# Two graph-attention and mixture-of-experts layers: rows scattered into expert regions while they are routed, engines in written order

## The chip, the cores and the metric

The kernel runs on one core of a Trainium2 chip. The metric is the device time of one execution in microseconds. The core has TensorE (PE, its weight loads shown apart as PEld), VectorE (DVE), ScalarE (ACT), GpSimd (POOL) and SyncE (SP); SP and POOL issue the transfers, which 16 DMA engines carry out.

## The reference, cut to what matters

There are 2708 rows of 256 features and a 2708 x 2708 adjacency. Every layer is an attention over the graph followed by a mixture of experts, each added to its input:

```python
# layer 0
x = x + gat(layernorm(x), adj)       # softmax over neighbours of leaky_relu(s_i + s_j), times h
x = x + moe(layernorm(x))            # 8 experts, 256 -> 1024 -> 256, gelu
# layer 1
x = x + hyperbolic_gat(layernorm(x), adj)   # W_gcn, W_att, per-row arccosh/sinh scalars, elu, sigmoid
y = n + moe(n), n = layernorm(x)     # 16 experts, 256 -> 512 -> 256, relu
x = x + layernorm(y) * gamma + beta
```

```python
def moe(x):                          # top-2 of E experts
    top_w, top_i = top_k(x @ Wg + bg, 2); top_w = softmax(top_w)
    return sum over k of top_w[k] * (act(x @ W1[top_i[k]] + b1) @ W2[top_i[k]] + b2[top_i[k]])
```

## The kernel before, in words

The rows are 22 tiles of 128 (the last has 20), used as 11 pairs. `x_all` holds them on the chip all the time.

Attention 0 (loop at L772 to L808). For each row tile, `mask_row` (DVE, L700) turns a row of the adjacency, loaded two tiles ahead, into a bf16 mask; `mask_turn` transposes it on PE (L709) and casts it on ACT (L712) into `mask_t`. For each pair and each source tile, `weigh` makes the weights (`zr` on ACT L722, `z` on DVE L725) and `gather` multiplies them on PE (L735). `close0` divides and adds; `turn0` applies the second layer norm, writes the row tile to DRAM (`rows_d`, SP, L357), transposes it, and `gate` gives the logits (L364).

The mixture of experts (`experts`, from L426). When all logits are there, a plan is computed at once for all rows: the two best experts by compares and reduces (L429 to L441), the rank of each row within its expert by products with a triangle matrix and with ones (L451, L455) and a scan (L461), the place of each row in blocks of 128 rows of one expert (L492 to L518), and the inversion, which gives for each place the row that goes there: 44 compares `in_block` (L523), each with a PE product (L525) with `which`. From it come `comes` and `goes`, the rows to read and the slots to write (L533 to L539). Biases are turned (L555), and `b2`, weighted by the gates, is added to every tile by a transpose (`wt_ps`, L567), a copy (L569), a product (`b_ps`, L571) and an add on DVE (L572). Then one loop over blocks (50 in layer 0, 58 in layer 1): `load` fetches the expert's weights on SP and the 128 rows by an indirect DMA on POOL (L589, three buffers); `hidden` transposes the rows, multiplies (L601) and applies the activation on ACT (L603); `outputs` multiplies (L611), copies on DVE (L614) and scatters to `outs_d` on POOL (L615). Lastly the combine loop fetches both results of each row as `two` (L640) and adds them, weighted (L645), to the accumulator.

Between the layers. `ready1` loads `w_gcn`, `W_att` and `a1_j` once the experts of layer 0 are done, and multiplies them into `w1x` (L846, L852). `project1` (L858) then takes each combined group through the layer norm, a transpose and a product with `w1x`. Per-row scalars follow for all tiles at once (L226 to L248), then attention 1 (L936 to L987): `widen` casts half a mask row on ACT (L938), `sum_up` multiplies (L946), `finish1` applies the elu. The sigmoid stage follows (L995, L998, L1004), the layer norm and routing rows of layer 1 (L1014 to L1021), the second mixture, and `finish` (L1023 to L1047), which normalizes each combined group of four tiles and writes it out.

What sets the order: a scheduler arranges the instructions of every engine by its own estimates of when their inputs are ready, within the order that the data allow. Groups of four tiles serve for the layer norms of L1014 and of the finish.

Of the kernel before, what the change touches and what calls it, by code (L numbers as in the profile page):

```python
# [32 lines left out]
def kernel(  # L33
# [25 lines left out]
    nc = tc.nc  # L59
    N, D = x.shape  # L60
# [6 lines left out]
    groups = [tiles[g:g + 4] for g in range(0, T, 4)]  # L67
# [62 lines left out]
    l0_scope = ExitStack()  # L130
    l0_pool = l0_scope.enter_context(tc.tile_pool(name="l0", bufs=1))
# [24 lines left out]
    nc.gpsimd.memset(minus_one, -1.0)  # L156
    nc.gpsimd.memset(mask_t[:, TF, :], 1.0)
# [13 lines left out]
    def score_weights():  # L171
        for c in range(DC):
            for k, (av, coef) in enumerate(((a0[1], 0.2), (a0[1], 0.8), (a0[0], 0.8))):
                junk = row_tile("junk", 2)
                nc.vector.scalar_tensor_tensor(
                    junk, w0_t[:, c, :D], coef, av, op0=OP.mult, op1=OP.mult,
                    accum_out=w0_t[:, c, D + k:D + k + 1])
# [6 lines left out]
    b2_0 = l0_pool.tile([E0, D], F32, name="b2_0")  # L184
    nc.gpsimd.dma_start(b2_0, L0_ffn_b2)
    b2_1 = const.tile([E1, D], F32, name="b2_1")
    nc.gpsimd.dma_start(b2_1, L1_ffn_b2)
    gamma = broadcast_rows("gamma", L1_ffn_gamma, 0, D)
    beta = broadcast_rows("beta", L1_ffn_beta, 0, D)
    b1_0 = l0_pool.tile([E0, L0_ffn_b1.shape[1]], F32, name="b1_0")  # L190
    nc.gpsimd.dma_start(b1_0, L0_ffn_b1)
# [115 lines left out]
    def ln_stats(ln, src, group):  # L307
# [7 lines left out]
        v, s, q = (stat()[:, :n] for _ in range(3))  # L315
        nc.vector.tensor_scalar(v, mv[:, lo:lo + n, 1], LN_EPS, None, op0=OP.add)
        nc.scalar.activation(s, v, AF.Sqrt)
        nc.vector.reciprocal(q, s)
        nc.vector.tensor_tensor(q, q, v, OP.mult)
        nc.vector.tensor_tensor(q, q, s, OP.add)  # L320
        nc.vector.tensor_scalar(q, q, 0.5, None, op0=OP.mult)
        nc.vector.reciprocal(rstd[:, lo:lo + n], q)
# [9 lines left out]
    def transpose_rows(dst, src, r):  # L332
# [4 lines left out]
        nc.scalar.copy(dst, ps[:, :DC, :r])  # L337
# [8 lines left out]
    class Router:  # L346


        def __init__(self, layer, E, w_gate, b_gate):
# [11 lines left out]
        def gate(self, t, r):  # L361
            ps = ps_wide("gate_ps")
            project(ps[:r, :self.E], self.xt.pop(t), self.w_gate, r)
            nc.vector.tensor_tensor(self.logits[:r, t, :], ps[:r, :self.E], self.b_gate[:r],  # L364
                                    OP.add)

# [710 lines left out]
```

## Time and profile before

| | us |
|---|---|
| median of three runs | 1458.45 (1456.02 to 1458.71) |
| profiled execution | 1459.07, its span 1457.3 |
| attention 0, PE without a gap | 30.5 to 332.7 |
| plan of layer 0 | 332.7 to 400.5 |
| expert blocks of layer 0 (50) | 400.5 to 765.4 |
| weights of layer 1, first `two` | 765.4 to 785.5 |
| combine, projection | 785.5 to 847 |
| scalars, mean | 847 to 885.5 |
| attention 1 | 885.5 to 1009.5 |
| sigmoid, scalars | 1009.5 to 1064 |
| rows, plan of layer 1 | 1064 to 1167.5 |
| expert blocks of layer 1 (58) | 1167.5 to 1389.8 |
| combine, finish | 1389.8 to 1457.3 |

PE is busy 81% of the span, DVE 40%, ACT 47%, POOL 16%; 248.46 MB are moved by DMA. Stages were read off the trace by the first and last instruction of each loop. The lines "busy tenths in 40 slices" cut the span into slices of 36.4 us, a digit of 9 is 90% or more; PEclk is the TensorE clock that was granted, in tenths. A line of windows gives, for one stretch, the busy time of each engine with the number of its instructions, the clock, the share of DMA and its rate.

### The profile page before, as it was taken

Reading aid. Unit: us, or ns where it says so; the run is one execution under the profiler, and the core shown is the slowest. Engines: PE = TensorE matmul, PEld = TensorE weight load, DVE = VectorE, ACT = ScalarE, POOL = GpSimd, SP = SyncE. Lnnn points to the kernel's source line nnn. Section 1 sums busy time; section 2 is a strip of 40 time slices with the busy share of each in tenths; the row PEclk is TensorE's granted clock in tenths of the full one; section 3 lists DMA queues with packets and bytes.
Section 4 is the critical chain, followed back from the end, with each engine's and each line's share of the span. In section 5 each row is a group of like instructions: output and inputs, shape, how many; then the busy total and the mean of one; then the engine's idle time right before and its main releaser. Section 6 shows DMA issues by size and latency. Waiting matters only on the chain. (4 is left out here: it accounts for less than half of the span.)

```text
span 1457.3 us, 21300 instructions
## 1 busy us (share of the span) xinstructions
PE 1184.7 (81%) x7294; PEld 1002.1 (69%) x7294; DVE 589.2 (40%) x1905; ACT 681.4 (47%) x1632; POOL 236.4 (16%) x297
## 2 busy tenths in 40 slices
PE   3999999993899999999992929997052999999910
PEld 2778888852599999999991408996051599999810
DVE  4756566637300000000004765566468501111179
ACT  3877777741144444444431546664611144444400
POOL 4000000000022222222211100000000045555400
PEclk9999999996599999999996969998555599999965
DMA  7313333000299999999963200000010199999943
GB/s 263 144 46 129 122 130 122 21 8 5 76 344 323 328 327 326 327 327 327 327 216 109 65 0 1 1 1 1 0 58 19 37 319 354 353 352 342 327 143 98
DMA packets 145181, 248.46 MB, mean 170 GB/s; under 512 B 9351, under 2 KB 102302, under 8 KB 142366
## 3 DMA queue, kind: packets, MB, share of 16 engines
q1 hardware_dynamic: 134354, 218.39, 43.3%
q0 software_dynamic: 10720, 28.72, 6.3%
q8 instruction: 58, 0.95, 0.3%
q14 instruction: 49, 0.40, 0.1%
HBM read 224.60 MB, written 22.47 MB: 170 GB/s over the span
## 5 line engine op out<-in xcount | busy, mean ns | idle before, releaser
L601 PEld LDWEIGHTS hid_ps<-xg_t,w_b 128*128 128x128 f32 x2528 | 301.3, 194 | 10.9 <-ACT xg_t L337 4.7
L611 PE MATMUL out_ps<-w_b,ht 128*128 128x256 f32 x1264 | 308.1, 380 | 0.0
L601 PE MATMUL hid_ps<-xg_t,w_b 128*128 128x128 f32 x2528 | 304.2, 277 | 1.8 <-ACT xg_t L337 1.0
L603 ACT ACTIVATE ht<-hid_ps,bias 128x128 f32<-128x128 f32 x632 | 232.2, 368 | 149.6 <-PE hid_ps L601 114.9
L614 DVE COPY yo<-out_ps 128x256 f32<-128x256 f32 x108 | 45.9, 425 | 548.2 <-PE out_ps L611 548.2
L735 PE MATMUL att_ps<-g_all,z 128*128 128x257 f32 x968 | 245.8, 391 | 0.6 <-DVE z L725 0.6
L611 PEld LDWEIGHTS out_ps<-w_b,ht 128*128 128x128 f32 x1264 | 224.3, 191 | 22.0 <-issue 0.2
L735 PEld LDWEIGHTS att_ps<-g_all,z 128*128 128x128 f32 x968 | 165.2, 185 | 42.6 <-issue 13.5
L589 POOL DMA_INDIRECT xg<-rows_d,comes x108 | 104.5, 967 | 477.8 <-PE tr_ps L336 314.6
L722 ACT ACTIVATE zr<-e_bc,minus_one,g_all 128x256 f32<-128x256 f32 (+1 forms) x242 | 139.9, 590 | 53.8 <-DVE z L725 52.0
L725 DVE SCALAR_TENSOR_TENSOR z<-zr,mask_t 128x256 f32<-128x256 f32 (+1 forms) x242 | 99.2, 410 | 92.5 <-PE att_ps L735 79.2
L946 PE MATMUL att_ps<-half,wide_mask 128*128 128x258 f32 x968 | 124.2, 287 | 0.0
L946 PEld LDWEIGHTS att_ps<-half,wide_mask 128*128 128x128 f32 x968 | 118.3, 188 | 6.2 <-issue 0.4
L615 POOL DMA_INDIRECT outs_d<-yo,goes x108 | 106.7, 988 | 71.4 <-issue 36.9
L337 ACT COPY xg_t<-tr_ps 128x256 f32<-128x256 f32 x108 | 40.2, 372 | 166.4 <-PE tr_ps L336 166.3
L468 POOL MEMSET edge<- 128x9 f32 (+1 forms) x2 | 0.2, 111 | 530.5 <-PE att_ps L735 314.0
L938 ACT CAST wide_mask<-mask_t 128x1408 fp32r<-128x1408 fp8e4 x44 | 59.9, 1368 | 45.2 <-PE att_ps L946 45.2
L712 ACT CAST mask_t<-mt_ps 128x1024 fp8e4<-128x1024 bf16 (+2 forms) x66 | 57.1, 871 | 24.4 <-PE mt_ps L709 24.2
L336 PE MATMUL tr_ps<-ident,y_all 128*128 128x128 f32 (+1 forms) x44 | 13.2, 426 | 62.9 <-DVE y_all L326 62.8
L709 PE MATMUL mt_ps<-ident_bf,mb 128*128 128x128 bf16 (+1 forms) x484 | 42.2, 226 | 17.8 <-DVE mb L700 16.8
L709 PEld LDWEIGHTS <-mb 128*128 128x128 bf16 (+1 forms) x484 | 34.3, 102 | 29.8 <-DVE mb L700 17.7
L336 PEld LDWEIGHTS tr_ps<-ident,y_all 128*128 128x128 f32 (+1 forms) x44 | 8.9, 251 | 63.8 <-DVE y_all L326 58.0
(288 smaller groups left out, 1179.3 us busy)
## 6 DMA issues: line engine op xcount, KB each, us to landing
w_b<-in_L_ffn_W_dram SPq DMA_DIRECT2D x100, 1024.0 KB, 9.3
w_b<-in_L_ffn_w_dram SPq DMA_DIRECT2D x116, 512.0 KB, 6.3
ad<-in_adj_dram SPq DMA_DIRECT2D x21, 1354.0 KB, 5.8
two<-outs_d SPq DMA_DIRECT2D x42, 256.0 KB, 2.9
rows_d<-xn SPq DMA_DIRECT2D x21, 128.0 KB, 1.7
rows_d<-y_all SPq DMA_DIRECT2D x21, 128.0 KB, 1.7
out_dram<-xn SPq DMA_DIRECT2D x21, 128.0 KB, 1.7
xg<-rows_d,comes POOLq DMA_INDIRECT x108, 6.1
```

Source lines behind the costliest of these rows:

```text
L589: nc.gpsimd.indirect_dma_start(out=xg, out_offset=None, in_=rows_d[:, :], in_offset=bass.IndirectOffsetOnAxis(ap=comes[:, b:b + 1], axis=0))
L601: nc.tensor.matmul(ps[:, :P], w1_b[:, c, f * P:(f + 1) * P], xt[:, c, :], start=(c == 0), stop=(c == DC - 1))
L603: nc.scalar.activation(ht[:, f, :], ps[:, :P], func, bias=bias[:, f, b:b + 1])
L611: nc.tensor.matmul(ps[:, :D], ht[:, f, :], w2_b[:, f, :], start=(f == 0), stop=(f == FC - 1))
L615: ins = nc.gpsimd.indirect_dma_start(out=outs_d[:, :], in_=yo, in_offset=None, out_offset=bass.IndirectOffsetOnAxis(ap=goes[:, b:b + 1], a ...
L709: nc.tensor.transpose(ps[:w, k, :r], mbs[i][:r, c * P:c * P + w], ident_bf[:r, :r])
L712: nc.scalar.copy(mask_t[:, lo:lo + full, i * P:i * P + r], ps[:, :full, :r], saturate=False)
L722: nc.scalar.activation(zr[:k, :n], e_bc[:k, lo:lo + n], AF.Relu, bias=minus_one[:k], scale=g_all[:k, j, D + 1:D + 2])
L725: nc.vector.scalar_tensor_tensor(z[:k, :n], zr[:k, :n], 1.0, mask_t[:k, j, lo:lo + n], op0=OP.add, op1=OP.mult)
L735: nc.tensor.matmul(accs[i][:r, :D + 1], z[:k, q * P:q * P + r], g_all[:k, j, :D + 1], start=(j == 0), stop=(j == TF))
L938: nc.scalar.copy(m, mask_t[:, part * HALF:(part + 1) * HALF, i * P:(i + 1) * P])
L946: nc.tensor.matmul(accs[i][:, :D + 2], wide_masks[i, j // HALF][:k, j % HALF, :], half[:k, j, :], start=(j == 0 and half is halves[0]), st ...
```

## The change

The order of PE, ACT, DVE and SP is now the order in which the program is written (`manual_schedule`); POOL's is still arranged. The program is rewritten to suit: `pipeline` runs the steps of successive pairs staggered, and attention 0 has an agenda that says after which of its steps each piece of other work is issued.

Routing is done pair by pair. In layer 0 the routing of a pair runs within the attention of the next one; in layer 1 it is a pipeline of six steps after the sigmoid stage. `pick` finds the two best experts, `rank` counts by three small products, `number` adds a running count per expert, and four indirect DMAs on POOL scatter the rows of the pair, each with its row and pair number in two extra columns (258 columns), into a region of 2816 rows per expert in DRAM. As the regions are only partly written, they are first filled with zeros by `clear` on SP: 22 fills of 9 x 128 rows of 1032 bytes (1.189 MB each) in layer 0, two behind each of the first eleven loads of the adjacency, and 22 of 17 x 128 rows (2.246 MB each) in layer 1, issued before attention 1.

The plan that remains computes for each block its expert and its first row in that expert's region; `comes` is a run of rows with a bound, so nothing is inverted. The slots to write are read from the extra columns of the gathered rows, two small DVE operations per block. The transposes and products of `b2` move into the first 22 blocks of the expert loop. The first two blocks are loaded ahead of the loop, `xg` has four buffers, and the weights of layer 1 are loaded and multiplied before the expert blocks of layer 0. Combine, projection and finish go by pairs, with `two` fetched two pairs ahead. The layer norm takes the square root with its epsilon on ACT and a correction step on DVE, per pair. In attention 1 the next mask is widened after the products of the present one. Attention 0 starts its first pair after 8 of the 22 front steps and has six buffers of z with a lag of four.

```diff
+    ctx.enter_context(tc.manual_schedule(engines={ET.PE, ET.Activation, ET.DVE, ET.SP}))
...
+    def pipeline(items, *steps):
+        for n in range(len(items) + len(steps) - 1):
+            for k in reversed(range(len(steps))):
+                if 0 <= n - k < len(items):
+                    steps[k](items[n - k])
...
-    def ln_stats(ln, src, group):
...
+    def ln_head(ln, src, group):
...
+        nc.scalar.activation(rstd[:, lo:lo + n], mv[:, lo:lo + n, 1], AF.Sqrt, bias=eps)
...
+        nc.vector.reciprocal(q, rstd[:, lo:lo + n])
+        nc.vector.tensor_tensor(w, q, q, OP.mult)
+        nc.vector.scalar_tensor_tensor(w, mv[:, lo:lo + n, 1], LN_EPS, w,
+                                       op0=OP.add, op1=OP.mult)
+        nc.vector.tensor_scalar(w, w, -0.5, 1.5, op0=OP.mult, op1=OP.add)
+        nc.vector.tensor_tensor(rstd[:, lo:lo + n], q, w, OP.mult)
...
-            self.rows_d = dram.tile([N, D], F32, name=f"rows_d{layer}")
...
-            nc.sync.dma_start(self.rows_d[t * P:t * P + r, :], xn)
...
+            self.rows_d = dram.tile([(E + 1) * LIMIT, RW], F32, name=f"rows_d{layer}")
...
+        def clear(self, k):
+            view = self.rows_d.rearrange("(e t p) d -> t p e d", e=self.E + 1, p=P)
+            for t in range(2 * k, 2 * k + 2):
+                ins = nc.sync.dma_start(
+                    view[t], nobody.unsqueeze(1).to_broadcast([P, self.E + 1, RW]))
+                for other in self.moves:
+                    tc.declare_no_dep(ins.ins, other, reason="a pair's tokens do not come that far")
+                self.fills.append(ins.ins)
...
+        def pick(self, pair):
+            E, lo, n = self.E, pair[0][0], len(pair)
+            hi = lo + n
+            order = rank[E].unsqueeze(1).to_broadcast([P, n, E])
+            seen = self.logits[:, lo:hi]
+            for k in range(2):
+                m = self.top[k]
+                nc.vector.tensor_reduce(m[:, lo:hi], seen, AX.X, OP.max)
...
+            both = row.tile([P, n, E], BF16, name="both", tag=f"both{E}", bufs=2)
+            nc.gpsimd.tensor_tensor(both, self.hot[:, lo:hi, 0], self.hot[:, lo:hi, 1], OP.add)
+            self.both = both
+            for t, r in pair:
+                nc.gpsimd.tensor_copy(self.rows[t][:r, D:D + 2], self.first[:r, t])
+        def rank(self, pair):
+            E, lo, n = self.E, pair[0][0], len(pair)
+            hi = lo + n
+            bank = ps_wide("rank_ps")
+            ps = bank[:, :2 * n * E].rearrange("p (t k e) -> p t k e", k=2, e=E)
+            sums = bank[:, 256:256 + n * E].rearrange("p (t e) -> p t e", e=E)
+            nc.tensor.matmul(ps, tri, self.hot[:, lo:hi], start=True, stop=False)
+            nc.tensor.matmul(ps[:, :, 1], ones_bf, self.hot[:, lo:hi, 0], start=False, stop=True)
+            nc.tensor.matmul(sums, ones_bf, self.both, start=True, stop=True)
+            self.ps[lo] = ps, sums
+        def number(self, pair):
+            E, lo, n = self.E, pair[0][0], len(pair)
+            hi = lo + n
+            ps, sums = self.ps.pop(lo)
+            at = row.tile([P, n, 2, E], F32, name="before", tag=f"before{E}", bufs=2)
+            for q in range(n):
+                nc.vector.tensor_tensor(at[:, q], ps[:, q],
+                                        self.count.unsqueeze(1).to_broadcast([P, 2, E]), OP.add)
+                nc.vector.tensor_tensor(self.count, self.count, sums[:, q], OP.add)
+            nc.vector.tensor_tensor(at, at, self.hot[:, lo:hi], OP.mult)
+            with nc.allow_low_precision(reason="whole numbers below 2 ** 24"):
+                nc.vector.tensor_reduce(self.place[:, lo:hi], at, AX.X, OP.add)
+            for t, r in pair:
+                for k in range(2):
+                    ins = nc.gpsimd.indirect_dma_start(
+                        out=self.rows_d[:, :], in_=self.rows[t][:r], in_offset=None,
+                        out_offset=bass.IndirectOffsetOnAxis(ap=self.place[:r, t, k:k + 1],
+                                                             axis=0))
+                    for other in self.moves:
+                        tc.declare_no_dep(ins.ins, other, reason="rows of different pairs")
+                    self.moves.append(ins.ins)
+                del self.rows[t]
...
-        in_block = gates.tile([P, G, P], BF16, name=f"in_block{layer}")
-        which = gates.tile([P, G, 2, NB], BF16, name=f"which{layer}")
-        nc.vector.tensor_tensor(which[:, :, 1, :], iota_b.unsqueeze(1).to_broadcast([P, G, NB]),
-                                place[:, 0].unsqueeze(2).to_broadcast([P, G, NB]), OP.is_equal)
-        nc.vector.tensor_tensor(which[:, :, 0, :], which[:, :, 1, :],
-                                tile_of.unsqueeze(2).to_broadcast([P, G, NB]), OP.mult)
-        for k in range(2):
-            nc.vector.tensor_scalar(which[:, k * T:(k + 1) * T, 1, :],
-                                    which[:, k * T:(k + 1) * T, 1, :],
-                                    pair_no[:, k:k + 1], None, op0=OP.mult)
-        ps = ps_wide("pair_ps")
-        for g in range(G):
-            nc.vector.tensor_scalar(in_block[:, g, :], iota_p, place[:, 1, g:g + 1], None,
-                                    op0=OP.is_equal)
-            nc.tensor.matmul(ps[:, :2 * NB], in_block[:, g, :],
-                             which[:, g].rearrange("p c b -> p (c b)"),
-                             start=(g == 0), stop=(g == G - 1))
...
-            ps = ps_wide("wt_ps")
-            nc.tensor.transpose(ps[:E, :r], wts[:r, t, :], ident[:r, :r])
-            wt = row.tile([E, P], F32, name=f"wt{layer}")
-            nc.scalar.copy(wt[:, :r], ps[:E, :r])
...
+        nc.vector.tensor_scalar(jump, need, -float(P), float(LIMIT), op0=OP.mult, op1=OP.add)
+        nc.gpsimd.memset(step_e, 2.0 ** 22)
+        nc.gpsimd.tensor_tensor(step_e[:, :E - 1], router.count[:, 1:], router.count[:, :E - 1],
+                                OP.subtract)
+        nc.gpsimd.tensor_scalar(end, router.count[:, 0:1], -1.0, None, op0=OP.add)
+        passed(row_f, jump)
+        passed(bound, step_e)
+        nc.vector.tensor_tensor(row_f, row_f, slots[:, :NB], OP.add)
+        nc.vector.scalar_tensor_tensor(comes, bound, end, row_f, op0=OP.add, op1=OP.min)
+        nc.vector.scalar_tensor_tensor(inside, bound, end, row_f, op0=OP.add, op1=OP.is_ge)
...
+            xg = pool.tile([P, RW], F32, name="xg", bufs=4)
+            ins = nc.gpsimd.indirect_dma_start(
+                out=xg, out_offset=None, in_=rows_d[:, :],
+                in_offset=bass.IndirectOffsetOnAxis(ap=comes[:, b:b + 1], axis=0))
+            for other in router.moves + router.fills:
+                tc.add_manual_dep(ins.ins, other.name, LANDED, reason="any pair's row")
+            return w1_b, w2_b, xg
...
+        held = [load(b) for b in range(2)]
...
+            goal = pool.tile([P, 1], I32, name="goal", bufs=3)
+            nc.vector.scalar_tensor_tensor(goal, xg[:, D + 1:D + 2], mine[:, b:b + 1],
+                                           xg[:, D:D + 1], op0=OP.not_equal, op1=OP.add)
+            nc.vector.copy_predicated(goes[:, b:b + 1], full[:, b:b + 1], goal)
...
+        aside()
+        xts, late = {0: turn(held[0][2])}, None
         for b in range(NB):
-            w1_b, w2_b, xg = load(b)
-            ht = hidden(b, w1_b, xg)
+            if b + 2 < NB:
+                held.append(load(b + 2))
+            w1_b, w2_b, xg = held.pop(0)
+            ht = hidden(b, w1_b, xts.pop(b))
+            if b + 1 < NB:
+                xts[b + 1] = turn(held[0][2])
             if late is not None:
                 outputs(*late)
-            late = (b, w2_b, ht)
+            late = (b, w2_b, xg, ht)
+            if 1 <= b <= T:
+                b2_add(*tiles[b - 1])
+            if b < T:
+                b2_turn(*tiles[b])
+                b2_evict(*tiles[b])
...
+        pipeline(pairs, fetch, lambda pair: None, combine, *after)
...
+        if i < len(pairs):
+            router0.clear(i)
...
+        steps = [(0, close0, pair), (2, lambda p: ln_tail(ln_f0, p), pair)]
+        for q, tl in enumerate(pair):
+            steps += [(3 + q, lambda p: turn0(*p), tl),
+                      (4 + q + LAG, lambda p: router0.evict(*p), tl)]
+        steps += [(7 + LAG, router0.gate, pair), (8 + 2 * LAG, router0.take, pair),
+                  (8 + 2 * LAG, router0.pick, pair), (12 + 2 * LAG, router0.rank, pair),
+                  (12 + 3 * LAG, router0.number, pair)]
...
+    LAG, FRONT = 4, 8
...
+    def load_weights(pool):
+        room = pool.tile([P, DC, 1024], F32, name="w1_b").rearrange("p c f -> p (c f)")
+        parts = {}
+        for name, lo, n in (("w_gcn", 0, D), ("w_gcn_t", 512, D), ("att_x", 1024, D + 1)):
+            parts[name] = room[:, lo:lo + DC * n].rearrange("p (c f) -> p c f", f=n)
+        parts["a1_j"] = room[:, 1600:1600 + D]
...
+        router1.clear(k)
...
+    widen(FIRST, 0)
+    widen(FIRST, 1)
     for i in range(FIRST, T):
-        for part in range(2):
-            widen(i, part)
-        finish1(*tiles[i - FIRST])
         for j in range(T):
             sum_up(i, j)
-    for i in range(T - FIRST, T):
-        finish1(*tiles[i])
+        if i + 1 < T:
+            widen(i + 1, 0)
+            widen(i + 1, 1)
+        if i == FIRST:
+            for old in range(FIRST - 1):
+                finish1(*tiles[old])
+        finish1(*tiles[i - 1])
+    finish1(*tiles[T - 1])
...
+    pipeline(pairs, lambda p: ln_head(ln_f1, x_tile, p), rows2, gate2, pick2, router1.rank,
+             router1.number)
...
+    def finish(pair):
+        ln_tail(ln_y, pair)
+        for t, r in pair:
+            o = row_tile("xn", 4)
+            ln_apply(o[:r], y_all[:r, t, :], ln_y, t, r)
             nc.vector.tensor_tensor(o[:r], o[:r], gamma[:r], OP.mult)
             nc.vector.tensor_tensor(o[:r], o[:r], beta[:r], OP.add)
             nc.vector.tensor_tensor(o[:r], o[:r], x_all[:r, t, :], OP.add)
             nc.sync.dma_start(out[t * P:t * P + r, :], o[:r])
```

## The prediction

> **What bounds the kernel now.** I read the page's slices first, to find the stages, then the windows cut along them, then the chain of waits for the two planning stages. From the page, busy tenths in 40 slices of 36.4 us, and the share of DMA:
>
> ```profile
> PE   3999999993899999999992929997052999999910
> DVE  4756566637300000000004765566468501111179
> PEclk9999999996599999999996969998555599999965
> DMA  7313333000299999999963200000010199999943
> ```
>
> PE is full in slices 1 to 8 (attention 0), 11 to 20 (FFN 0), 24 to 27 (attention 1) and 32 to 37 (FFN 1). Between them the granted clock falls to 0.5 and nothing is full: these are the stages that the change rewrites. The windows; columns are stretch, length, busy time of PE, PEld, DVE, ACT and POOL, clock, DMA share, GB/s:
>
> ```profile
> 0.00:39.00 39.00, 15.18 (x94) 11.60 (x94) 18.61 (x69) 14.64 (x26) 15.83 (x47) 1.00 0.77 273
> 115.00:165.00 50.00, 50.00 (x304) 41.91 (x303) 32.16 (x91) 37.81 (x69) 0.00 (x0) 1.00 0.37 135
> 333.00:399.30 66.30, 39.44 (x143) 23.84 (x142) 40.75 (x146) 9.90 (x37) 3.19 (x5) 0.52 0.11 36
> 540.00:610.00 70.00, 70.00 (x481) 65.34 (x480) 4.25 (x10) 31.60 (x86) 18.07 (x19) 1.00 0.93 330
> 765.00:785.00 20.00, 4.85 (x12) 3.23 (x12) 0.94 (x5) 2.68 (x5) 3.22 (x7) 0.66 0.19 56
> 785.00:847.00 62.00, 46.07 (x132) 21.38 (x132) 48.97 (x187) 26.51 (x119) 6.50 (x23) 0.89 0.29 85
> 1102.00:1167.00 65.00, 36.16 (x127) 20.98 (x124) 45.03 (x131) 8.65 (x30) 2.92 (x3) 0.50 0.08 27
> 1240.00:1310.00 70.00, 70.00 (x491) 65.18 (x490) 7.64 (x18) 34.64 (x94) 36.70 (x38) 1.00 1.03 354
> 1390.00:1457.30 67.30, 0.00 (x0) 0.00 (x0) 59.27 (x212) 1.23 (x6) 0.85 (x2) 0.53 0.41 126
> ```
>
> Both planning stages (333 to 399, 1102 to 1167) are serial work on DVE and PE with the DMAs idle. FFN 0 is PE's (70 of 70). FFN 1 is PE's and the DMAs' together (70 of 70, 354 GB/s). The last stage is DVE's (59 of 67). The chain of waits names what each planning stage ends with, and what follows FFN 0:
>
> ```profile
> 768.93 8.15 DMA w_gcn<-in_L_gnn_W_gcn_dram
> 1148.60 5.41 PE b_ps L571 x12
> 1155.18 4.56 PE b_ps L571 x10
> 1161.48 4.71 DMA xg<-rows_d,comes
> ```
>
> So the b2 products and then the first gather (4.71 us) end the plan, and a weight load of 8.15 us stands behind FFN 0. The sum below is against the profiled execution: 1459.07 us, span 1457.3, 1.8 around it; the median of the runs is 0.6 less.
>
> **Plan 0 (332.7 to 400.5, 67.8 us): -36.** Removed from this path: 44 in_block compares with their matmuls, the two which products, the scan, b2. What stays after the last attention matmul, in order: the rank and number of pair 9, which written order puts ahead of the last close, delay it by 2.1; close, LN, transposes, gate and logits 6.7 (10 or so dependent steps of 0.2 to 0.5 with one table load of 1.28); pick 2.4 (12 small DVE steps at 0.2); rank 1.0; number 1.2 (6 steps); four scatters on POOL at 0.97 and about 2.2 to land (5 us in all for one at 1389.8: issue 0.97, the fetch behind it starts 2.6 after), 6.1; gather 1.0 + 4.7; transpose and copy 1.2. That is 26.4. The bias transposes (5.3 in before) and the w_gcn products (1.08 + 3.77 in before) are written ahead of the first block on PE; about half falls beside the scatters and gather: 5 to 6. So 32 in place of 67.8. Bounds: 26 if all of it hides, 42 if none does and the weights for block 0 (9.3 from issue to landing, after the plan) come last. On SP the loads of b2, b1, w_gcn, W_att and a1_j now stand ahead of the first expert's weights; they need only the attention's buffers and go out while the last pair is routed, so I charge nothing; were that cover gone, the 8.15 us of w_gcn would come before the weights, inside the 42. On POOL the gathers stand behind the four scatters, which is counted.
>
> **FFN 0 (365 us): +18.** b2 moves into its first 22 blocks, where PE is full, so nothing covers it. A product is two records of 217 ns warm (a 256-column f32 record), a transpose 0.11, and two changes of operand shape: 0.09 to 0.15 each time where such a change shows: 0.85 per tile, 22 of them 18.7. Bounds: 0.54 each (12) and 1.1 (24: a cold record is 427 ns). The first blocks' cold start is as before. Gathers on POOL are issued two blocks ahead; xg has four buffers: no charge, the cover is 7.25 us per block against 1 + 4.7. If that cover goes, each block loses its gather wait.
>
> **After FFN 0 (765.4 to 785.5): -14.** w_gcn is loaded and multiplied before FFN 0. What is left is the last scatter's landing and `two` (1.0 + 2.4 + 2.6), 5.6 to 6. **Combine 0 and projection (62 us): +2.** DVE per pair, at start-to-start gaps: combine 4 x 0.39, head 1.08, LN tail 1.0, apply 0.65, keep 0.67: 4.98, eleven times 55; PE needs 46. Filling and draining a five-step pipeline takes about 9. **Scalars (847 to 872.6): -5**: four wide_mask casts of 1.36 on ACT are no longer written ahead of them. **Attention 1 (124.67 of 125 on PE): 0**: the same 968 records; its casts have 2.8 us per half-row on ACT. The end loses one finish of two: **-2**.
>
> **Rows and routing 1 (1064 to 1167.5): -8.** Here DVE carries it all: head 1.08, tail 1.0, apply 0.65, logits 0.15, pick 2.4 (E is 16, a little longer), number 1.3: 6.0 to 6.6 per pair, 66 to 73 for eleven; fill 10; and behind the last number four scatters, the plan (three pairs of passes over 128 x 928 at 1.04 each beside them), gather and transposes, 15. 95 against 103.5. Bounds 86 and 112 (a dependent step at 0.32, as the reciprocal, in place of 0.2).
>
> **FFN 1 (222 us): +14.** The same 18.7 of b2; but 222.3 less 58 blocks of 3.73 leaves 6 us of waits for weights, and more PE time per block hides most of those: 18.7 - 4.7. Bounds +8 and +22.
>
> **Finish (1390 to 1457): +17.** Before, tiles of a group are interleaved by the scheduler, so four 256-wide steps are 0.33 apart. Written order goes apply, gamma, beta, x for one tile and then the other, each waiting for the one before it: 0.44 (dependent TENSOR_TENSORs at the end of before: 1453.75, 1454.19, 1454.63). Per pair: tail 1.0 (five steps, where before six steps served four tiles), eight steps 3.3 (0.33 to 0.44 mixed), head 1.08, combine 1.58: 6.96, eleven 76.6 against 59.6. Bounds +8 (all at 0.33) and +24.
>
> **Attention 0 (0 to 332.7): -2.** Eight tiles' front in place of the whole one starts pair 0 about 8.7 sooner; DVE then stands in written order at the mask row of adj 2, landing at 31; three rank matmuls for each of ten pairs add 4 on PE. Per pair PE has 22.7 us, DVE about 20 and ACT 20 with the routing added. The scatters (4 on POOL) are off the path.
>
> **The fills.** Layer 0 writes 22 x 1.189 MB on SP's queue, two behind each of the first eleven adj loads (1.387 MB). Each mask row then asks 3.76 MB of the queue in 11.35 us, 331 GB/s. Rates seen: 273 (start), 330 (FFN 0), 354 (FFN 1). At 331 or more nothing is lost, and I take that, since the FFN rows carry 1 KB packets too, most of the page's 102302 packets under 2 KB. At 273 it is 13.8 us per row: 9 rows x 2.4 = +22; at 250, +33. Writes to DRAM at such rates are not in this trace, so the lower ends stay in the range.
> [...]
> Layer 1's fills, 49.4 MB, start behind the `two` fetches at about 805 and must land by the first scatter, near 1046: 206 GB/s, with the queue otherwise empty (1 GB/s in attention 1). No charge; at 170 GB/s, the mean over the span, 49.4 MB take 291 us: +45.
>
> **The sum:** -2 -36 +18 -14 +2 -5 -2 -8 +14 +17 = -16: 1443 us. [...]
>
> **The rivals.**
> 1. Slower: the layer 0 fills hold back adj. Place: mask_row on DVE, which in written order also holds z and with it PE. [...] Against: 354 seen. It decides below about 300 GB/s for the fills; 1465 to 1476.
> 2. Slower or none: convoys. Engines in written order wait for each other where the scheduler would have gone around; attention 0 has 2 to 3 us of slack per pair on DVE and ACT. At 1.5 to 3 us per pair, +15 to +30: 1458 to 1473.
> 3. The late layer 1 fills: up to 1488.
> 4. Faster: b2 at its lower bounds in both FFNs (-12) and the finish at 0.33 per step (-9): about 1422.
> 5. The change does not take the plan off the path: the plan of before stays 60 us or so because the gather waits for all scatters and fills. Against: the layer 0 fills end 200 us earlier. Counted with 3.
>
> **How the numbers follow.** Forecast 0.45, rival 1 0.20, rival 2 0.15, rival 4 0.14, rivals 3 and 5 0.06. A run of this kernel can tell about 0.2% (2.9 us) from no change. The forecast's own errors of some 15 us put 0.38 of its 0.45 on the faster side; rival 4 adds 0.14, a mild convoy 0.06: 0.58. Within 0.2%: 0.06. Slower: 0.36. The forecast's own range is 1425 to 1460; with rivals 4 and 1 to 3 it is 1412 to 1488.
>
> **What would show it.** Right: the first hid_ps of FFN 0 comes 30 to 35 us after the last att_ps of attention 0; FFN 0 some 383 long, with wt_ps and b2_ps records in its first 22 blocks alone; no w_gcn in the chain after FFN 0; a DVE-bound end of 75 us. Wrong: DVE's mb waiting for ad after 40 us (rival 1); idle PE inside attention 0 released by z with no DMA behind it (rival 2); POOL's first layer 1 scatter waiting for a fill (rival 3).

## The result and the profile after

The changed kernel takes 1541.47 us (median of 4 runs, 1540.77 to 1546.25) against 1458.58 before (median of 4): a ratio of 1.058, 95% interval 1.055 to 1.060. I forecast 1443 with a range up to 1488; it is slower by 83 us. The profiled execution has a span of 1539.2 us, 81.9 more than before. Stages below are read from one profiled execution of each kernel.

The page after, busy tenths in 40 slices, now of 38.5 us each:

```profile
PE   4588998989399999999995649884044599999700
...
DVE  4446666674411111110117765556388422211298
ACT  4556657664144444444443455553610244444300
...
PEclk9789999999599999999997969997555699999955
DMA  9639973210388888999974999991002588999731
```

Slices are counted from 0. Before, PE stood at 9 in all of slices 1 to 8. Now it has a 5 in slice 1 and 8s among the 9s in slices 2 to 8 (attention 0), and 8s in slices 25 and 26 (attention 1), while DVE and ACT are no fuller: PE loses time to engines that are not busy. The DMA row shows the fills: 7 to 9 in slices 3 to 5, 9 in slices 22 to 26.

The two traces by stage, from the first and last PE record of each loop:

| stage | before | after | change | forecast |
|---|---|---|---|---|
| attention 0, up to its end | 333.2 | 389.4 | +56.2 | -2 |
| plan 0, to the first block | 67.3 | 37.8 | -29.5 | -36 |
| expert blocks of layer 0 | 364.2 | 381.6 | +17.4 | +18 |
| weights, combine, projection, scalars | 108.1 | 97.6 | -10.5 | -17 |
| mean and attention 1 | 136.8 | 150.9 | +14.1 | 0 |
| sigmoid, rows, routing 1, to the first block | 157.8 | 157.2 | -0.6 | -10 |
| expert blocks of layer 1 | 221.6 | 237.7 | +16.1 | +14 |
| combine and finish | 68.3 | 87.2 | +18.9 | +17 |

So the 98 us between -16 and +82 lie in attention 0 (58), in attention 1 (14), and in three stages that gained less than forecast (6.5, 6.5 and 9.4); the other three stages are within 2.5 us of their terms. Windows of the changed kernel; columns are stretch, length, busy time of PE, PEld, DVE, ACT and POOL, clock, DMA share, GB/s:

```profile
20.00:40.00 20.00, 15.46 (x90) 11.37 (x88) 11.30 (x34) 14.66 (x31) 0.00 (x0) 1.00 0.97 266
40.00:60.00 20.00, 7.83 (x33) 5.79 (x34) 10.04 (x31) 9.50 (x20) 0.00 (x0) 0.74 1.08 293
60.00:80.00 20.00, 12.50 (x55) 9.34 (x54) 8.96 (x31) 9.80 (x20) 0.00 (x0) 0.78 0.06 16
...
104.00:389.40 285.40, 262.64 (x1488) 206.23 (x1486) 178.27 (x580) 179.21 (x337) 71.42 (x66) 0.98 0.51 150
...
918.30:1057.20 138.90, 125.53 (x969) 118.31 (x968) 79.76 (x153) 70.74 (x109) 1.94 (x4) 1.00 0.98 235
```

In the front (20 to 80 us) no engine is busy more than four fifths of a row, and between 60 and 80 us hardly a transfer runs either (16 GB/s): what is left as the bound is the chain between the engines, which the experiments test. From 104 us on, PE is idle for 23 of 285 us; in attention 1 for 13 of 139, over the same work as before (124.17 busy of 124.20). What PE and ACT wait for, from the waits of these stretches (engine, first instruction after the wait, what ended it; us in all, times, longest):

```profile
PE tr_ps L347 <- DVE xr L337: 20.1, 10, 2.2
```

```profile
ACT junk L1073 <- DVE rinv L1063: 56.3, 18, 3.1
```

The first is attention 0: ten times, once per pair, PE stands some 2 us at the transposes of the routed rows until DVE has written them, with the products of z tiles that are ready standing behind. The second is attention 1: ACT stands 3.1 us per tile at the square that ends `finish1`.

### The profile page after: what moved, and what is told of

It reads as the page before. It is cut to its first block, busy times and chain, and to the rows that moved or that the text cites. A ratio compares the mean times of both kernels' runs of the same rounds, so it can differ in the third digit from the quotient of the medians.

```text
span 1539.2 us, 21883 instructions
## 1 busy us (share of the span) xinstructions
PE 1173.6 (76%) x7264; PEld 991.6 (64%) x7264; DVE 686.3 (45%) x2385; ACT 674.7 (44%) x1648; POOL 366.8 (24%) x461
## 5 line engine op out<-in xcount | busy, mean ns | idle before, releaser
L649 PEld LDWEIGHTS hid_ps<-xg_t,w_b 128*128 128x128 f32 x2528 | 297.1, 193 | 8.3 <-ACT xg_t L351 3.1
L664 PE MATMUL out_ps<-w_b,ht 128*128 128x256 f32 x1264 | 290.4, 379 | 0.0
L664 PEld LDWEIGHTS out_ps<-w_b,ht 128*128 128x128 f32 x1264 | 231.9, 190 | 27.2
L810 PE MATMUL att_ps<-g_all,z 128*128 128x257 f32 x968 | 240.8, 394 | 0.0
L810 PEld LDWEIGHTS att_ps<-g_all,z 128*128 128x128 f32 x968 | 172.8, 189 | 41.5 <-issue 16.3
L797 ACT ACTIVATE zr<-e_bc,minus_one,g_all 128x256 f32<-128x256 f32 (+1 forms) x242 | 134.6, 587 | 42.8 <-DVE z L800 42.2
L492 POOL DMA_INDIRECT rows_d<-xr,place x44 | 50.5, 1147 | 117.5 <-DVE z L800 54.8
L632 ACT COPY wt<-wt_ps 8x128 f32<-8x128 f32 (+3 forms) x44 | 11.0, 251 | 125.4 <-PE wt_ps L628 125.4
L347 PE MATMUL tr_ps<-ident,xn 128*128 128x128 f32 (+1 forms) x88 | 18.0, 314 | 54.2 <-DVE xn L337 39.4
L321 ACT ACTIVATE rstd_f<-mv_f,eps 128x2 f32<-128x2 f32 x22 | 6.5, 296 | 112.0 <-DVE mv_f L319 112.0
```

The lines of the kernel that those rows point to most:

```text
L347: nc.tensor.transpose(ps[:, c, :r], src[:, c * P:(c + 1) * P], ident[:r, :r])
L649: nc.tensor.matmul(ps[:, :P], w1_b[:, c, f * P:(f + 1) * P], xt[:, c, :], start=(c == 0), stop=(c == DC - 1))
L664: nc.tensor.matmul(ps[:, :D], ht[:, f, :], w2_b[:, f, :], start=(f == 0), stop=(f == FC - 1))
L797: nc.scalar.activation(zr[:k, :n], e_bc[:k, lo:lo + n], AF.Relu, bias=minus_one[:k], scale=g_all[:k, j, D + 1:D + 2])
L810: nc.tensor.matmul(accs[i][:r, :D + 1], z[:k, q * P:q * P + r], g_all[:k, j, :D + 1], start=(j == 0), stop=(j == TF))
```

## The experiments

Each changes one thing of the changed kernel unless its text says otherwise, and was run once unless an interval is given. Two theories to begin with: the written order makes engines wait in turn (my rival 2, "convoys"), or the zero fills hold the adjacency back (my rival 1).

**Fills spread out.**

```diff
-        if i < len(pairs):
-            router0.clear(i)
+        if i % 2:
+            router0.clear(i // 2)
```

> The 22 zero fills of layer 0 go out behind every second adjacency load over the whole of attention 0 instead of behind each of the first eleven, so that the queue is asked for about 227 GB/s instead of 331. Nothing else is moved. If the fills hold the adjacency back (my first rival), attention 0, which now ends at 389.4, ends 20 to 35 us earlier and the whole is near 1510. If the written order of the engines is what holds it (each waiting in turn for another), the end of attention 0 moves by less than 5 us and the whole stays near 1541.

Measured: 1541.73 us, the end of attention 0 at 389.1 (389.4). Rival 1 falls: the fills are not what delays attention 0. In the kernels with scheduled engines below, adjacency and fills together run at 302 to 336 GB/s between 20 and 78 us, and the pair's period does not show it.

**The turn of the routed rows later.** The square root on ACT goes from step 0 of the agenda to 2, the normalised rows from 3 to 5, their transposes from 3 to 8, the correction steps behind the root by two steps, the rest by three or four.

```diff
-        steps = [(0, close0, pair), (2, lambda p: ln_tail(ln_f0, p), pair)]
+        steps = [(0, close0, pair), (2, lambda p: ln_root(ln_f0, p), pair),
+                 (4, lambda p: ln_tail(ln_f0, p), pair)]
...
-            steps += [(3 + q, lambda p: turn0(*p), tl),
-                      (4 + q + LAG, lambda p: router0.evict(*p), tl)]
+            steps += [(5 + q, lambda p: turn0(*p), tl),
+                      (8 + q, lambda p: router0.turn(*p, xrs.pop(p[0])), tl),
+                      (8 + q + LAG, lambda p: router0.evict(*p), tl)]
```

> Within the agenda of attention 0 the square root of the layer norm on ACT is written two steps later, the normalised rows two steps later and their transposes on PE five steps later; the rest of the routing moves by three steps. If the written order costs the loop its 27.35 us per pair (24.07 before), because PE stands 2.17 us per pair at the transposes until DVE has the rows, the period falls to about 24.7 and attention 0 ends 20 to 25 us earlier, near 366; the whole is near 1519. If the fills or the three rank products are what costs, the period stays above 27.

Measured: 1521.0 us, attention 0 ends at 370.4, 19.0 earlier. The period in the middle of the loop (mean of seven) is 25.26 us; 27.55 in the changed kernel, 24.07 before. The wait named above is gone, and the largest one in its place is a new one of the same kind, PE for the mask rows:

```profile
PE mt_ps L785 <- DVE mb L775: 8.7, 8, 1.2
```

So two thirds of what the loop lost is one chain in the written order; the rest moves to the next such place. All of that chain was moved (the root on ACT, the rows on DVE, the transposes on PE), and ACT's wait in front of the root fell too, from 37.8 to 18.5 us: how the gain divides between the two waits was not tried.

**The front's rows ahead.**

```diff
-    LAG, FRONT = 4, 8
+    LAG, FRONT = 4, 9
...
             if 1 <= t <= T:
-                front_sum(*tiles[t - 1])
+                front_turn(*tiles[t - 1])
             if 2 <= t < T + 2:
-                front_project(*tiles[t - 2])
...
+                front_keep(*tiles[t - 2])
+            if 3 <= t < T + 3:
+                front_sum(*tiles[t - 3])
+                front_project(*tiles[t - 3])
```

> In the front of attention 0 the normalised row tile is written one step ahead of its transposes, and the copy of the transposes one step behind them, so that no step has the whole chain row, transpose, copy, weight, z, next row in it. If that chain is what makes a front step 3.4 us long, the last projection (103.5 now, 86.0 before) ends 15 to 25 us earlier and so does the whole, near 1521. If the transfers of the start hold the front (fills and adjacency at 266 to 299 GB/s until 60 us), it stays within 5 us of 103.5.

Measured: 1539.12 us, the last projection at 102.3 (103.5). A miss for my account of the chain: but for one wait at the start (12.1 us) the transposes do not wait for the rows any more, and yet the front is only 1.2 us shorter. The waits of its first 110 us say which chain is left: ACT for the projections, PE for ACT's copies.

```profile
ACT g_all L763 <- PE h_ps L355: 34.9, 21, 3.4
DVE e_bc L774 <- PE e_ps L770: 25.2, 10, 5.3
...
PEld h_ps L355 <- ACT xt L746: 16.1, 10, 4.4
PE h_ps L355 <- ACT xt L746: 13.4, 8, 4.0
```

**Everything scheduled.**

```diff
-    ctx.enter_context(tc.manual_schedule(engines={ET.PE, ET.Activation, ET.DVE, ET.SP}))
```

> The one line that fixes the order of PE, ACT, DVE and SP as written is taken out; all else of the change stays, fills included. If the written order is what costs, attention 0 goes back to about 24.5 us per pair and ends near 340, attention 1 to about 125 us (139 now), and the whole is near 1541 - 50 - 14 = 1477. If the fills or the added routing work cost attention 0 its 56 us, it still ends above 370 and the whole is above 1510.

Measured: 1441.31 us beside 1460.25 for the kernel before on the same chip (one run each). That is 100 us less than the changed kernel, by one line, and 19 less than before. By stage (table below): attention 0 ends at 328.8 in place of 389.4, with a period of 24.15, so the added routing costs PE 0.1 us per pair; attention 1 takes 124.2; the combine stages, routing 1 and the finish gain 11 to 17 each. Plan 0 and the expert loop of layer 0 are 6.7 and 8.8 worse.

**The elu's second half later.** `finish1` is cut behind its tanh; the rest is `close1`.

```diff
+        close1(*tiles[i - 2])
         finish1(*tiles[i - 1])
...
+    close1(*tiles[T - 2])
+    close1(*tiles[T - 1])
```

> In attention 1 of the changed kernel finish1 is cut after its tanh, and its second half (DVE steps and the square on ACT) is written one tile later. If ACT stands 3.1 us per tile at the square while the next two mask casts (2.7 us) stand behind it, 6.3 us per tile in place of the 5.64 that PE needs, attention 1 goes from 138.9 to about 125 us; the stage behind it gains up to 3 us for the second half that is left over; the whole is 10 to 14 us faster, near 1529. If the zero fills of layer 1, which run beside it, or something else holds it, it stays near 139.

Measured: 1526.84 us, attention 1 takes 124.2 (138.9), to the tenth what it took before the change. ACT's instructions in one tile of the changed kernel (start us, us, instruction, and in brackets the idle time before it with its releaser), and then of this one:

```profile
1004.27 0.42 ACT L1073 ACTIVATE junk<-h_all 128x255 f32<-128x255 f32 x1 [3.13 <-DVE rinv L1063]
1004.60 0.18 ACT L1073 ACTIVATION_READ_ACCUMULATOR junk<-h_all 128x1 f32 x1
1004.69 2.62 ACT L1044 CAST wide_mask<-mask_t 128x1408 fp32r<-128x1408 fp8e4 x2
1007.21 0.41 ACT L1067 ACTIVATE lo<-lo 128x256 f32<-128x256 f32 x1
1010.75 0.42 ACT L1073 ACTIVATE junk<-h_all 128x255 f32<-128x255 f32 x1 [3.13 <-DVE rinv L1063]
```

```profile
1002.67 1.37 ACT L1044 CAST wide_mask<-mask_t 128x1408 fp32r<-128x1408 fp8e4 x1 [1.46 <-PE att_ps L1052]
1003.94 0.41 ACT L1080 ACTIVATE junk<-h_all 128x255 f32<-128x255 f32 x1
1004.26 0.19 ACT L1080 ACTIVATION_READ_ACCUMULATOR junk<-h_all 128x1 f32 x1
1004.35 0.40 ACT L1069 ACTIVATE lo<-lo 128x256 f32<-128x256 f32 x1
1005.50 1.37 ACT L1044 CAST wide_mask<-mask_t 128x1408 fp32r<-128x1408 fp8e4 x1 [0.75 <-PE att_ps L1052]
```

In the first, the mask casts stand behind 3.13 us of waiting, and a tile takes 6.48 us (from square to square) where PE needs 5.64. In the second, ACT waits for PE.

**The finish's tiles alternate.**

```diff
...
+        for by in (gamma, beta):
+            for o, (t, r) in zip(os, pair):
+                nc.vector.tensor_tensor(o[:r], o[:r], by[:r], OP.mult if by is gamma else OP.add)
...
```

> In the finish of the changed kernel the four 256-wide steps of the two tiles of a pair are written alternately, so that no step directly follows the one that it needs. By my term for the finish (0.44 for a dependent step, 0.33 for an independent one, 8 steps in each of 11 pairs) the last stage goes from 87.2 to 78 to 80 us. If the order within the pair is not what costs and the waits of the pipeline's steps for ACT's square root and the fetches are, it stays above 85.

Measured: 1533.75 us, the last stage 79.1 (87.2). The changed kernel's DVE, where each step needs the one before it, and this kernel's, pairs of steps joined in one line:

```profile
1492.08 0.41 DVE L337 TENSOR_SCALAR xn<-y_all,mv_y,rstd_y 128x256 f32<-128x256 f32 x1
1492.53 0.43 DVE L1154 TENSOR_TENSOR xn<-xn,gamma 128x256 f32<-128x256 f32 x1
1492.99 0.43 DVE L1155 TENSOR_TENSOR xn<-xn,beta 128x256 f32<-128x256 f32 x1
1493.45 0.43 DVE L1156 TENSOR_TENSOR xn<-xn,x_all 128x256 f32<-128x256 f32 x1
```

```profile
1489.94 0.73 DVE L337 TENSOR_SCALAR xn<-y_all,mv_y,rstd_y 128x256 f32<-128x256 f32 x2
1490.60 0.75 DVE L1156 TENSOR_TENSOR xn<-xn,gamma 128x256 f32<-128x256 f32 x2
1491.27 0.75 DVE L1156 TENSOR_TENSOR xn<-xn,beta 128x256 f32<-128x256 f32 x2
```

0.46 per dependent step (1492.53, 1492.99, 1493.45), and 0.67 for two that alternate, 0.335 each.

**Without b2 in the loops.**

```diff
-            if 1 <= b <= T:
-                b2_add(*tiles[b - 1])
-            if b < T:
-                b2_turn(*tiles[b])
-                b2_evict(*tiles[b])
```

> The b2 terms (transpose, copy, product, add for 22 tiles) are left out of both expert loops of the changed kernel; that part of the computation is missing. By my terms (0.85 us of PE per tile, 18.7 per layer) the loop of layer 0 goes from 381.6 to 363 and that of layer 1 from 237.7 to 219 to 224. If written order or the second small DVE steps per block cost these loops instead, less than half of that comes back.

Measured: 1504.81 us; the loop of layer 0 takes 363.4 (381.6), that of layer 1 220.9 (237.7): 18.2 and 16.8, or 0.83 and 0.76 per tile. On balance nothing else of the written order costs these two loops: they are at or below the 364.2 and 221.6 of before.

**Written order in the experts alone.**

```diff
-    ctx.enter_context(tc.manual_schedule(engines={ET.PE, ET.Activation, ET.DVE, ET.SP}))
...
+        written = ExitStack()
+        written.enter_context(tc.manual_schedule(engines={ET.PE, ET.Activation, ET.DVE, ET.SP}))
         early(pool)
...
         outputs(*late)
+        written.close()
```

> The order is as written only from the plan of each layer to the last block of its expert loop; everything else (both attentions, combine, scalars, routing of layer 1, finish) is arranged by the scheduler. If written order is worth something only where the scheduler lost against it (plan 0 44.5 against 37.8, expert loop of layer 0 390.4 against 381.6, of layer 1 240.4 against 237.7), the whole is 1441 - 18 = 1423, attention 0 ending at about 329. If the gains and losses of the two orders are tied to each other across stages, it stays at 1436 or more.

Measured: 1454.92 us, far above the 1423; a miss. Attention 0 ends at 340.3, plan 0 takes 53.3, the loop of layer 0 389.3 with written order inside. The longest wait of PE there is for a weight that SP had issued:

```profile
PE bias_ps L598 <- DMA w_b<-in_L_gnn_W_att_dram: 31.1, 1, 31.1
```

From 330 to 420 us the queue moves 271 GB/s at a DMA share of 0.95. Where SP is arranged by the scheduler, it issues the fills of layer 1 not behind combine 0, where they are written, but from 158 us on here (154 with everything scheduled): of the 49.4 MB all but two fills of 2.2 MB stand in front of the weights of layer 0. The next run tests that reading.

**SP alone in written order.**

```diff
-    ctx.enter_context(tc.manual_schedule(engines={ET.PE, ET.Activation, ET.DVE, ET.SP}))
+    ctx.enter_context(tc.manual_schedule(engines={ET.SP}))
```

> Only SP issues in written order; PE, ACT and DVE are arranged by the scheduler. With all four arranged, SP issued the layer 1 fills from 154 us on, and the last scatters of layer 0 landed 10.8 us late behind them; here they stand where they are written, behind the fetches of combine 0. If that traffic is what makes plan 0 44.5 and the expert loop of layer 0 390.4 us there, they go to about 35 to 38 and 382, and the whole is near 1441 - 16 = 1425. If the scheduler's order of the other engines is the reason, those stages stay and the whole is 1438 or more.

Measured: 1418.96 us against 1460.14 for before on the same chip, ratio 0.972 (0.970 to 0.974): faster than both kernels. Plan 0 takes 34.7 and the loop of layer 0 380.9, as expected. DVE's wait for the last scatters, which opens the plan, shows the fills' part; with everything scheduled, and with SP written:

```profile
DVE have L528 <- DMA rows_d<-xr,place: 10.8, 1, 10.8
```

```profile
DVE have L529 <- DMA rows_d<-xr,place: 5.9, 1, 5.9
```

Its front, for the same stretch as above, has DVE and ACT fuller throughout and PE from 40 us on, at full clock and with the same transfers running faster:

```profile
20.00:40.00 20.00, 15.09 (x89) 12.29 (x90) 17.52 (x69) 15.03 (x33) 0.00 (x0) 1.00 1.07 329
40.00:60.00 20.00, 19.42 (x112) 15.18 (x112) 15.38 (x42) 18.75 (x45) 0.00 (x0) 1.00 1.07 302
60.00:77.40 17.40, 17.34 (x89) 13.31 (x88) 10.43 (x25) 12.25 (x34) 0.00 (x0) 1.00 1.07 320
77.40:327.70 250.30, 250.30 (x1450) 197.47 (x1449) 168.94 (x574) 178.76 (x327) 53.00 (x66) 1.00 0.51 159
```

**b2 moved**, on top of SP alone in written order. In layer 1 PE adds row tile and b2 product in PSUM, and combine reads the sum from there:

```diff
+                    nc.tensor.matmul(sums[t], ident[:r, :r], acc_all[:r, t, :], start=True, stop=False)
+                    nc.tensor.matmul(sums[t], wt_sb.pop(t)[:, :r], b2, start=False, stop=True)
...
+        if layer == 0:
+            for tl in tiles[:8]:
+                b2_turn(*tl)
+                b2_evict(*tl)
+                b2_add(*tl)
```

> As the run beside it with only SP written, and b2 moved: in layer 1 out of the expert loop into the last stage, where PE is idle; PE adds the row tile and the b2 product in PSUM there, so that DVE does no more; in layer 0 the first 8 tiles of b2 are written ahead of the first block, where PE waits for the scatters and the gather. By 0.85 us per tile in a full PE this gives 18 us in layer 1 and up to 7 in layer 0: 1400 to 1405. If the last stage pays for it (PSUM operands, cold products of 0.43 per record in the way of DVE) it gains less than 10.

Measured: 1409.18 us, ratio 0.964 (0.963 to 0.966), 9.8 us less than the run beside it and not the 18 to 25 expected. Layer 1 gives 18.5 in its loop (220.1) and pays 3.5 in the last stage; in layer 0 the loop gains 4.2 and plan 0 loses 9.3. So it is plan 0, more than the last stage, that keeps the gain under 10.

**b2 of layer 1 alone moved.** As above, without the 8 tiles ahead of the first block of layer 0.

> Only SP in written order, and b2 of layer 1 alone moved into the last stage; b2 of layer 0 stays in its first 22 blocks, since writing 8 tiles of it ahead of the first block cost plan 0 9.3 us and gave the loop 4.2. Expected: plan 0 back at 35, the loop of layer 0 at 381, the loop of layer 1 at 220 and the last stage at 73: 1407 - 5 = 1402 for the span, about 1404 in all. If the 9.3 us of plan 0 came from elsewhere, it stays at 1409.

Measured: 1412.95 us (1406.29 to 1416.12), ratio 0.967 (0.964 to 0.969). Plan 0 (34.6) and the loop of layer 0 (380.9) came as expected, but the loop of layer 1 took 226.2 and the routing 3.7 more, with PE waiting for expert weights eight times (3.3 us) and once 8.0 us for gathered rows. Its interval overlaps the one before it, so these runs do not say which of the two is better.

**The front alone.**

```diff
-    LAG, FRONT = 4, 8
+    LAG, FRONT = 4, 26
```

> In the changed kernel, all engines in written order, the first pair's weights and products begin after the whole front (26 steps) in place of after 8. The front then has no zr and z between a tile's copy and the next tile's row. If these close the chain that makes its steps 3.4 to 4.2 us long, the last projection comes from 103.5 to 80 or earlier and the pair then takes its 27 us behind it: the end of attention 0 moves from 389.4 to 370 to 395, mostly unchanged in sum. If PE and ACT wait for each other in the front without them (two PSUM buffers shared by transposes and projections, both copies read by ACT in the same step), the last projection stays above 92 and attention 0 ends later than 395.

Measured: 1539.83 us; the last projection at 80.3 (103.5), the end of attention 0 at 387.3 (389.4). So the first pair's work (zr, z, its products, and the next pair's masks, which move with them) is what stretched the front by about a quarter. Starting that pair 18 steps earlier gained almost nothing in the end: done alone, its products take 24.3 us (85.1 to 109.4) and end 6.9 earlier than in the changed kernel (116.3), of which the ten pairs behind lose 4.9 again (277.9 for 273.0).

The stages of the kernels that decide (us):

| stage | before | after | all scheduled | SP written | b2 moved |
|---|---|---|---|---|---|
| attention 0, up to its end | 333.2 | 389.4 | 328.8 | 327.7 | 329.0 |
| plan 0 | 67.3 | 37.8 | 44.5 | 34.7 | 44.0 |
| expert blocks 0 | 364.2 | 381.6 | 390.4 | 380.9 | 376.7 |
| weights, combine, scalars | 108.1 | 97.6 | 86.1 | 87.4 | 88.0 |
| mean and attention 1 | 136.8 | 150.9 | 135.7 | 136.3 | 136.3 |
| sigmoid, routing 1 | 157.8 | 157.2 | 143.0 | 140.2 | 140.0 |
| expert blocks 1 | 221.6 | 237.7 | 240.4 | 238.6 | 220.1 |
| combine and finish | 68.3 | 87.2 | 70.4 | 69.4 | 72.9 |

## Why the prediction was wrong, by its own steps

- **Attention 0 (-2): this step failed; +56.** I set "DVE about 20 and ACT 20" against PE's 22.7 us per pair and took the slack as enough. A sum of busy times bounds an engine that takes its work as it comes; in written order every wait of one engine stands in front of its next instruction too, as ACT's 3.13 us do in front of the mask casts in attention 1. The 22.7 was itself low: the period before was 24.07. PE stood 20.1 us at ten transposes, and moving the chain that ends in them took 19.0 off. Of the 56, 30 are the ten pairs after the first (some 3 each) and 26 the first pair with the front. I had charged the front nothing but a mask row and let it start "pair 0 about 8.7 sooner"; the first product came at 60.5 us, 21.3 later than before (39.2). With the first pair's work in it, the front's steps close a chain across PE, ACT and DVE.
- **The rivals.** The right mechanism was rival 2, at a chance of 0.15 and +15 to +30. Its rate per pair (1.5 to 3) was close, at 3.0 on average, but I confined it to the loop of attention 0. It was also in the front (26), in attention 1 (14), and in the stages that gained less. Taking the order away gave 100 us. Rival 1, which I held likelier, is excluded by the spread fills. Rivals 3 and 5 did not occur in the changed kernel: the last fill was issued at 1021 us, some 26 from landing, and the first scatter of layer 1 at 1138. (At 170 GB/s rival 3 would have been 291 us against 241, so 50 and not my 45.) The fills of layer 1 did collide, but only where the scheduler was free to issue them early. Rival 4 fails on b2 (16.8 to 18.2) and on the finish.
- **Attention 1 (0): failed, +14.** I counted "2.8 us per half-row on ACT" for its casts and left out the elu's square behind a 3.1 us chain on DVE, which written order puts ahead of the next casts.
- **Finish (+17): right in size, +18.9, and in cause for the dependent steps.** The term of 0.44 against 0.33 per step was 0.46 against 0.335; alternating gave 8.1 back, close to the 9 that I had put on it. The other +8, which I put on the work of a pair itself, is mostly order too: the scheduler's order gives 17 back with the same steps and leaves +2.1. That this part came out is luck.
- **b2 (+18 and +14): right, +17.4 and +16.1**, and 18.2 and 16.8 by leaving it out: 0.83 and 0.76 us per tile, beside my 0.85, in loops at a clock of 1.00 and 0.99 (0.52 and 0.50 in the plans of before).
- **Plan 0 (-36): right in kind, -29.5.** The chain took 37.8 where I summed 32. With SP alone written it is 34.7.
- **After the expert loop of layer 0 to the scalars (-17) and routing 1 with the sigmoid stage (-10): right for the program, not for its order.** The changed kernel gave -10.5 and -0.6; SP alone written gives -20.7 and -17.6. That the order is the difference is shown; which wait in these stages costs what was not tried one by one and stays open.
- **The sum.** With all engines scheduled the same program took 1441.31, beside my 1443. That is not the forecast coming true: the forecast was for the written order, and the nearness is a sum of misses both ways. The finish (+2.1 for +17), the combine stages (-22 for -17) and routing (-14.8 for -10) were better than I had summed, plan 0 (-22.8 for -36) and the loops (+26.2 for +18, +18.8 for +14) worse. What shows that the order was mis-sized, and not the scatter into regions, is the 100 us between two kernels that differ by that one line.
- **The fills of layer 0 (no charge): right.** No run shows a delay by them: with the fills in the queue 302 to 336 GB/s were moved in the two kernels with scheduled engines, below the 354 of the expert loop of layer 1, and spreading them left the end of attention 0 at 389.1 (389.4). Fills with the queue to themselves were slower still: those of layer 1 moved 261 GB/s in the changed kernel (930 to 1020 us) and 295 with SP alone written (850 to 930), both at a DMA share of 1.09, where the loop's 354 had 1.03. What makes that difference was not tried.

## What to carry to other kernels

Before an order is fixed by hand, write out for each engine what stands behind each of its waits; an engine's busy share says nothing of that, and a stage that was bound by one full engine loses whatever its engine waits for others (PE was idle for 23 us in attention 0 and for 13 in attention 1). The waits view of the bound engine and of the engine that it waits for, cut to one stage, shows such places, and shifting the waiting work behind work that is ready (by two to five steps in attention 0, one tile in attention 1) gave back 19.0 and 14.7 us. In the front it did not: the one shift tried there only moved the wait. Order can be fixed per engine: here the queue of transfers was worth fixing (the scheduler sent some 45 MB of fills ahead of the weights), while the computing engines were better left to the scheduler.

## What the runs showed of the hardware that I had not expected

The convoys of attention 0 made themselves dearer. PE's waits in the loop of attention 0 lasted 2.2 us at most, yet behind three of the ten the granted clock stood at half for 3.4 us. Windows of these three and of the loop, and then of the loop with the turn later:

```profile
149.70:153.10 3.40, 3.40 (x14) 2.54 (x13) 1.91 (x2) 2.57 (x7) 0.00 (x0) 0.51 1.09 287
204.30:207.70 3.40, 3.40 (x15) 2.55 (x14) 1.97 (x5) 1.89 (x5) 0.00 (x0) 0.50 1.10 295
286.20:289.60 3.40, 3.30 (x14) 2.57 (x14) 1.83 (x6) 2.05 (x5) 2.54 (x3) 0.50 0.22 78
116.30:389.40 273.10, 250.34 (x1419) 196.41 (x1418) 171.39 (x565) 168.49 (x317) 71.42 (x66) 0.98 0.52 154
```

```profile
118.00:370.40 252.40, 243.73 (x1419) 192.90 (x1418) 168.66 (x565) 162.59 (x316) 57.05 (x66) 1.00 0.54 167
```

The same 1419 records of PE took 6.6 us less at a clock of 1.00 in place of 0.98, about a third of the 20.7 that the loop gained. In the front, with PE idle more than half of the stretch from 40 to 60 us, the clock was 0.74, and a projection's record (`h_ps`) took 0.52 us on average, against 0.40 before, where the clock was 1.00 there. What that adds to the front is open: with the fills spread out the clock was 0.58 there, and the last projection came only 1.4 us later.

The expert loop of layer 1 took 220.1 us in one profile and 226.2 in another, of kernels that differ elsewhere, at a DMA share of 0.96 and 0.95; the second has the waits for weights and rows named above. Why they fell in the one and not in the other is open.
